# Turned squares of softmax probabilities sent from SBUF straight to SBUF in a fused attention and MLP kernel

## The chip, the cores and the metric

The kernel runs on one core of one Trainium2 chip. The metric is the device time of one execution in microseconds; the time before is the median of three runs.

## The reference

The input is 16 sequences of 256 tokens of width 256. Attention has 16 heads of 128; the MLP is 2048 wide, with 4-bit weights. In the reference's terms:

```python
x = x + layernorm(attention(layernorm(x)))      # causal softmax, 16 heads, biases on q, k, v, out
x = x + layernorm(mlp(layernorm(x)))            # out = (gelu(x Wg) * (x Wu)) Wd

scores = einsum('bqhe,bkhe->bhqk', q, k) / sqrt(128)
attn   = softmax(where(causal, scores, -1e5), axis=-1)
z      = einsum('bkhe,bhqk->bqhe', v, attn)
out    = einsum('bqhe,hed->bqd', z, W_O) + b_O
```

`Wg`, `Wu` and `Wd` are unpacked from 4-bit codes, one scale for every 32 values.

## The kernel before, in words

The 4096 tokens are cut into 8 blocks of 512 (two sequences). Attention goes over *units*: a unit is one block and one head, so there are 128 of them, and two units of neighbouring heads make a *pair* (64 pairs). Almost every product is made of several matmuls on high and low parts of the operands, to keep float32 accuracy.

A software pipeline, written out by hand, is the loop `for i in range(-5, N + 2)` with N = 128. In step `i` these stages are recorded, in this order: `st_s(i+4)` (scores and softmax), `st_qk(i+5)` (keys and queries), `st_t(i+4)`, in the last steps a `part` of the MLP's first group, `st_o` (output projection of an earlier pair), `st_z(i)` (values times probabilities), `st_p(i+1)`, `st_v(i+4)` (values), `st_b(i+3)`, `st_w(i+4)` and then `weights`, which loads weight tiles for later pairs: `wo` and `wv` in odd steps, `wk` and `wq` in even ones. In between, `slot` calls take small jobs from queues: layernorms of other blocks, the splitting of weights, the unpacking of the 4-bit weights.

The helper `run` (line 99) chains every engine instruction behind those recorded before it, and the helper `dma` (lines 86 to 91) does the same for all transfers, which are all issued by SyncE (SP) in the order in which they are recorded. So nothing overtakes on an engine or in SP's queue: a transfer that has to wait holds up all transfers recorded after it. In the built program each transfer also carries one of eight completion counters in turn, and waits until the transfer eight places before it has landed.

The probabilities must be turned (transposed) before `st_z` can use them. For one unit this goes in four stages:

- `st_t`: VectorE transposes the 32 by 32 squares of `pr` into `tr`, 128 partitions by 768 elements.
- `st_w`: `spread` stores `tr` in a DRAM tile `hop`, in four transfers of 32 partitions and 96 KB each. They put the squares where the transposed matrix has them.
- `st_b`: one transfer of 384 KB loads `hop` into the SBUF tile `pt`, of which there are three buffers.
- `st_p`: ScalarE copies the high part `ph` out of `pt`, GpSimd (in the last four units VectorE) makes the low part `pl`. `st_z` reads `ph`, `pl` and a part of `pt` itself on TensorE.

Unit `u` is stored in step `u-4`, loaded in step `u-3`, split in step `u-1` and used in step `u`.

The 4-bit weights are unpacked during attention (`f_make`, `f_scale`) and kept in DRAM (`f_keep`); the second loop, over MLP groups `k`, loads them again (`f_get`). Its tiles are `wg`, `wu` and `wd`. Its first group begins inside the last attention steps.

Of the kernel before, what the change touches and what calls it, by code (L numbers as in the profile page):

```python
# [10 lines left out]
F32 = mybir.dt.float32  # L11
F32R = mybir.dt.float32r
I32 = mybir.dt.int32
BF16 = mybir.dt.bfloat16
AF = mybir.ActivationFunctionType
ALU = mybir.AluOpType

B, S, D, H, E, FF = 16, 256, 256, 16, 128, 2048
P = 128
# [9 lines left out]
def kernel(  # L29
# [19 lines left out]
    nc = tc.nc  # L49
# [4 lines left out]
    wp = ctx.enter_context(tc.tile_pool(name="w", bufs=2))  # L54
    work = ctx.enter_context(tc.tile_pool(name="work", bufs=2))
    small = ctx.enter_context(tc.tile_pool(name="small", bufs=3))
    dram = ctx.enter_context(tc.tile_pool(name="dram", bufs=1, space=bass.MemoryType.DRAM))
    ps = ctx.enter_context(tc.tile_pool(name="ps", bufs=1, space=bass.MemoryType.PSUM))

    def f(ap):  # L60
        return ap.bitcast(F32)
# [24 lines left out]
    def dma(dst, src):  # L86
        if queue[0] is None:
            queue[0] = nc.sync.dma_start(dst, src).ins
            return
        with tc.issue_after(queue[0]):  # L90
            queue[0] = nc.sync.dma_start(dst, src).ins
# [3 lines left out]
    def run(op, dst, *args, **kw):  # L95
        with ExitStack() as behind:
            for m in last.values():
                behind.enter_context(tc.issue_after(m))
            ins = op(dst, *args, **kw)  # L99
        last[ins.ins.engine] = ins.ins  # L100
        return ins
# [3 lines left out]
    V_, G_, A_, N_ = "vgan"  # L105
    urgent, behind, splits, idle, made, spare = (deque() for _ in range(6))
# [91 lines left out]
    def spread(hop, tr):  # L198

        to = hop.rearrange("(k j) a n -> a j k n", k=4)  # L200
        for a in range(4):
            dma(to[a], tr[32 * a : 32 * (a + 1)])
# [161 lines left out]
    N = len(units)  # L364
# [95 lines left out]
    def st_t(u):  # L460


        pr = PR.pop(u)
        tr = work.tile([P, 4, 6, 32], F32, tag="tr", name="tr")
        run(
                nc.vector.transpose,
                tr.rearrange("p k m i -> p m k i"), pr.rearrange("p c b (k j) -> p (c b) k j", k=4)
            )
        TR[u] = tr

    def st_w(u):
        HOP[u] = dram.tile([P, 4, 6 * 32], F32, tag="hop", name="hop", bufs=4)
        spread(HOP[u], TR.pop(u).rearrange("p k m i -> p k (m i)"))

    def st_b(u):

        pt = work.tile([P, 4, 6, 32], F32, tag="pt", name="pt", bufs=3)
        dma(pt.rearrange("p a m i -> p a (m i)"), HOP.pop(u))
        PT[u] = pt

    def st_p(u):
        pt = PT.pop(u).rearrange("p a m i -> p m a i")
        ph = work.tile([P, 2, 2, P], F32R, tag="ph", name="ph")
        pl = work.tile([P, 2, 2, P], F32R, tag="pl", name="pl")
        four = [t.rearrange("p c b (a i) -> p (c b) a i", a=4) for t in (ph, pl)]
        run(nc.scalar.copy, four[0], pt[:, 0:4])

        engine = nc.vector if u >= N - 4 else nc.gpsimd
        run(engine.tensor_tensor, four[1], pt[:, 0:4], f(four[0]), ALU.subtract)
        PH[u] = (ph, pl, pt)  # L490
# [127 lines left out]
    def f_make(g, n, then):  # L618


        pk, sc = LD.pop((g, n))

        def small_tile(dtype, name):
            return work.tile([P, 2, 256], dtype, tag="code", name=name, bufs=3)

        c = work.tile([P, 2, 256], I32, tag="raw", name="codes", bufs=6)
        sg, t = small_tile(BF16, "sg"), small_tile(BF16, "t")
        run(nc.vector.tensor_scalar, c[:, 0, :], pk, 15, None, ALU.bitwise_and)
        run(nc.vector.tensor_scalar, c[:, 1, :], pk, 4, 15, ALU.arith_shift_right, ALU.bitwise_and)
        yield V_  # L630
        if then:
            f_load(*then)
        run(nc.vector.tensor_scalar, sg, c, 8.0, -2.0, ALU.is_ge, ALU.mult)
        yield V_
        run(nc.vector.tensor_scalar, c, c, 7, None, ALU.bitwise_and)
        yield V_
        run(nc.vector.tensor_scalar, t, c, 2.0, 8.0, ALU.mult, ALU.subtract)
        yield V_
        while unscaled:
            step(made)  # L640
        v = small_tile(BF16, "v")
        run(nc.vector.scalar_tensor_tensor, v, c, 0.5, t, ALU.mult, ALU.max)
        yield V_
        run(nc.vector.scalar_tensor_tensor, v, c, 2.0, v, ALU.subtract, ALU.max)
        yield V_
        run(nc.vector.scalar_tensor_tensor, v, sg, 1.0, v, ALU.add, ALU.mult)
        unscaled.append((g, n))
        add(made, f_scale(g, n, v, sc), G_)

    def f_scale(g, n, v, sc):  # L650
        scb = sc.unsqueeze(1).to_broadcast([P, 2, 256])
        if n == "d":
            full = work.tile([P, 2, 256], F32, tag="raw", name="full", bufs=6)
            w = f_tile(n)
            run(nc.gpsimd.tensor_tensor, full, v, scb, ALU.mult)
            unscaled.remove((g, n))
            yield A_
            run(nc.scalar.copy, w[:, 0], full)
            run(nc.gpsimd.tensor_tensor, w[:, 1], full, f(w[:, 0]), ALU.subtract)
        else:  # L660

            full = work.tile([P, 8, P], F32, tag="eight", name="full", bufs=1)
            run(nc.gpsimd.tensor_tensor, full[:, 0:4].rearrange("p (k c) n -> p k (c n)", k=2), v, scb, ALU.mult)
            unscaled.remove((g, n))
            w = f_tile("u")
            yield A_
            run(nc.scalar.copy, w[:, 0, 0:4], full[:, 0:4])
            run(nc.gpsimd.tensor_tensor, w[:, 1, 0:4], full[:, 0:4], f(w[:, 0, 0:4]), ALU.subtract)
            yield G_
            a11, a21, a12, a22, s1, s2, s3, s4 = (full[:, m] for m in range(8))  # L670
            for o, l, r, op in (
                (s1, a21, a22, ALU.add), (s2, s1, a11, ALU.subtract), (s3, a11, a21, ALU.subtract),
                (s4, a12, s2, ALU.subtract),
            ):
                run(nc.gpsimd.tensor_tensor, o, l, r, op)
            yield A_
            run(nc.scalar.copy, w[:, 0, 4:8], full[:, 4:8])
            run(nc.gpsimd.tensor_tensor, w[:, 1, 4:8], full[:, 4:8], f(w[:, 0, 4:8]), ALU.subtract)
        late.append((now[0] + 4, f_keep, (g, n, w)))

    def f_tile(n):
        if n == "d":
            return wp.tile([P, 2, 2, 256], F32R, tag="fd", name="wd", bufs=2)
        if n == "g":
            return wp.tile([P, 2, 1024], F32R, tag="wv", name="wg", bufs=2).rearrange("p s (m c) -> p s m c", m=8)
        return wp.tile([P, 2, 8, P], F32R, tag="fs", name="wu", bufs=2)
# [336 lines left out]
    for i in range(-5, N + 2):  # L1023
        p = i // 2
        odd = i % 2 == 1
        if p >= 0 and not odd and p < len(pairs):
            b, g = pairs[p]
            if g == 0 and b + 1 < NBLK:
                add(urgent, ln1(b + 1), N_)
            if b == 0 and g == 6:  # L1030
                pieces = [(fg, n) for fg in range(NG) for n in "gud"]
                f_load(*pieces[0])
            if b == 0 and g == 7:
                for m, piece in enumerate(pieces):
                    add(idle, f_make(*piece, pieces[m + 1] if m + 1 < len(pieces) else None), V_)
            if b == NBLK - 1 and g == 0:
                add(spare, x_ops(0), N_)
        if 0 <= i + 4 < N:
            st_s(i + 4)
        slot(V_)  # L1040
        if i + 5 < N:
            st_qk(i + 5)
        slot(V_, urgent, behind)
        slot(G_)
        slot(G_)
        if 0 <= i + 4 < N:
            st_t(i + 4)
        if i == N:
            await_(X[0], "last", spare)
            X[0].pop("last")()  # L1050
        if i >= N - 4:
            part(0, ("m1", "m2", "m6", "m5", "m7", "m3")[i - (N - 4)])
        if 0 <= p - 1 < len(pairs):
            st_o(p - 1, i % 2)
        if 0 <= i < N:
            st_z(i)
        if 0 <= i + 1 < N:
            st_p(i + 1)
        if 0 <= i + 4 < N:
            st_v(i + 4)  # L1060
        elif after:
            run(*after.popleft())
        if 0 <= i + 3 < N:
            st_b(i + 3)
        if 0 <= i + 4 < N:
            st_w(i + 4)
        if odd:
            weights((p + 1, "o"), (p + 5, "v"))
        else:
            weights((p + 4, "k"), (p + 4, "q"))  # L1070
        slot(A_ + G_)
        if N - 9 <= i < N - 7:
            f_get(0, "ug"[i - (N - 9)])
# [97 lines left out]
```

## Time and profile before

| | |
|---|---|
| time, median of 3 runs | 1518.19 us (1518.02 to 1520.27) |
| profiled execution, first to last instruction (its span) | 1516.5 us |
| profiled execution's own time outside the span | not recorded apart; the median of the runs is 1.7 us above the span |
| TensorE matmul busy | 1500.2 us, 99% |
| VectorE, ScalarE, GpSimd busy | 1188.5, 1038.3, 724.5 us |
| transfers' share of the 16 DMA engines, 200 to 1000 us | 0.91 to 0.94 |
| the same, 1200 to 1500 us | 0.51 to 0.61 |
| mean granted TensorE clock | 0.998 |

PE is TensorE's matmuls and PEld its weight loads, DVE is VectorE, ACT ScalarE, POOL GpSimd; SPq is SyncE's queue, which issues the transfers. The last attention step's products end at about 1023 us of the span; the MLP goes on to its end. Idle time of an engine that sets no end costs nothing, so the waits that matter here are those of PE.

### The profile page before, as it was taken

To read this page: it belongs to the slowest core of one execution; us is meant where nothing else is said; L and a number is where in the kernel's file an instruction comes from. 1 tells how busy PE (TensorE), PEld (TensorE's weight loads), DVE (VectorE), ACT (ScalarE), POOL (GpSimd) and SP (SyncE) were. 2 spreads that over 40 slices of the span, in tenths; PEclk is the share of its full clock that TensorE was granted. 3 is DMA by queue.
4 is the path that set the end of the run, shared out by engine and by line. 5 is a ranking of instruction groups with operands and counts; after the bars stand their busy time and mean duration, and the time that the engine had idled before them with its cause. 6 is when DMAs were issued, how large, how long until landed. Compare 5 with 4: busy or idle time off the path is not lost.

```text
span 1516.5 us, 25756 instructions
## 1 busy us (share of the span) xinstructions
PE 1500.2 (99%) x7831; PEld 1278.8 (84%) x7831; DVE 1188.5 (78%) x3015; ACT 1038.3 (68%) x2614; POOL 724.5 (48%) x947
## 2 busy tenths in 40 slices
PE   8999999999999999999999999999999999999997
PEld 7888888888888888888888888887888888888886
DVE  6876787787787878788778787777787887787866
ACT  6887776776676677676677767676766665666565
POOL 3754578677767776866876876870000000000000
PEclk9999999999999999999999999999999999999999
DMA  8998899999999899899899999976557465655561
GB/s 289 333 328 260 261 307 305 291 303 313 285 296 322 279 320 309 273 316 302 280 286 320 298 297 318 318 253 259 209 194 261 183 248 196 249 182 196 221 233 58
DMA packets 200426, 407.55 MB, mean 269 GB/s; under 512 B 21472, under 2 KB 128480, under 8 KB 189536
## 3 DMA queue, kind: packets, MB, share of 16 engines
q1 hardware_dynamic: 200288, 405.91, 80.0%
q8 instruction: 62, 1.02, 0.3%
q14 instruction: 76, 0.62, 0.1%
HBM read 294.15 MB, written 111.67 MB: 268 GB/s over the span
## 4 chain that ended last, share of the span: by engine, by line
PE 92%; DVE 2%; DMA 2%; ACT 2%; POOL 1%; issue 1%; SPq 0%; POOLq 0%; DVEq 0%; ACTq 0%
PE pd L99 13%; PE pk L99 11%; PE pv L99 11%; PE pq L99 11%; PE po L99 11%; PE sc L99 9%; PE pz L99 9%; PE pa L99 8%; PE pf L99 5%; PE pe L99 2%; DMA wu<-fu 1%; DVE sum L99 1%; ACT pr L99 0%; DMA rawv<-in_wv 0%; PE warm L99 0%
## 5 line engine op out<-in xcount | busy, mean ns | idle before, releaser
L99 POOL TENSOR_SCALAR pr<-pr,rc 128x128 f32<-128x128 f32 (+1 forms) x512 | 251.1, 508 | 90.1 <-DVE rc L99 90.1
L99 ACT ACTIVATE pr<-sc,mn 128x128 f32<-128x128 f32 (+1 forms) x512 | 208.8, 420 | 87.1 <-DVE mn L99 87.0
L99 POOL TENSOR_TENSOR rs<-rs,mhalf 128x4 f32<-128x4 f32 (+1 forms) x35 | 34.5, 987 | 485.6 <-DVE rs L99 275.7
L99 POOL TENSOR_TENSOR pl<-pt,ph 128x512 fp32r<-128x512 f32 x124 | 160.0, 1290 | 186.5 <-ACT ph L99 178.2
L99 DVE CUSTOM_DVE_ANT_0 sc<-sc,mask 128x128 f32<-128x128 f32 (+1 forms) x512 | 180.7, 373 | 68.0 <-PE sc L99 59.2
L99 PE MATMUL pv<-wv,xT 128*128 128x512 f32 x768 | 208.9, 407 | 0.0
L99 ACT ACTIVATE zh<-pz,bqk 128x512 fp32r<-128x512 f32 x128 | 88.3, 690 | 165.1 <-PE pz L99 165.1
L99 PE MATMUL pk<-xT,wk 128*128 128x512 f32 x768 | 200.3, 396 | 0.3 <-POOL xT L99 0.2
L99 PE MATMUL pd<-inter,wd 128*128 128x512 f32 (+1 forms) x792 | 197.8, 385 | 1.4 <-ACT inter L99 1.0
L99 PE MATMUL pq<-xT,wq 128*128 128x512 f32 x768 | 196.3, 391 | 0.0
L99 PEld LDWEIGHTS pd<-inter,wd 128*128 128x128 f32 x792 | 145.0, 188 | 34.5 <-DVE inter L99 2.9
L99 PEld LDWEIGHTS pq<-xT,wq 128*128 128x128 f32 x768 | 144.2, 188 | 32.9
L99 ACT COPY part<-pa 128x512 f32<-128x512 f32 x192 | 111.9, 586 | 68.4 <-PE pa L99 66.0
L99 PE MATMUL po<-zh,wo 128*128 128x512 f32 x512 | 157.7, 389 | 0.0
L99 PEld LDWEIGHTS pk<-xT,wk 128*128 128x128 f32 x768 | 135.7, 189 | 24.0 <-POOL xT L99 0.7
L99 PEld LDWEIGHTS pv<-wv,xT 128*128 128x128 f32 x768 | 135.0, 189 | 23.6
L99 DVE SCALAR_TENSOR_TENSOR zl<-pz,bqk,zh 128x512 fp32r<-128x512 f32 x128 | 95.8, 749 | 70.5 <-ACT zh L99 70.5
L99 ACT CAST inter<-sum 128x512 fp32r<-128x512 f32 x128 | 80.1, 626 | 87.9 <-DVE sum L99 87.9
L99 DVE TENSOR_TENSOR inter<-sum,inter 128x512 fp32r<-128x512 f32 x128 | 89.0, 695 | 56.9 <-ACT inter L99 56.0
L99 DVE STREAM_TRANSPOSE tr<-pr 128x768 f32<-128x768 f32 x128 | 123.3, 963 | 1.7 <-POOL pr L99 1.2
L99 DVE SCALAR_TENSOR_TENSOR kl<-pk,bqk,kh 128x512 fp32r<-128x512 f32 x128 | 96.1, 751 | 30.9 <-ACT kr L99 27.1
L99 PEld LDWEIGHTS po<-zh,wo 128*128 128x128 f32 x512 | 96.0, 188 | 19.9
(150 smaller groups left out, 3726.1 us busy)
## 6 DMA issues: line engine op xcount, KB each, us to landing
hop<-tr SPq DMA_DIRECT2D x512, 96.0 KB
pt<-hop SPq DMA_DIRECT2D x128, 384.0 KB
wk<-wk SPq DMA_DIRECT2D x64, 512.0 KB
wq<-wq SPq DMA_DIRECT2D x64, 512.0 KB
wo<-wo SPq DMA_DIRECT2D x64, 512.0 KB
wu<-fu SPq DMA_DIRECT2D x32, 1024.0 KB
wg<-fg SPq DMA_DIRECT2D x32, 1024.0 KB
wv<-wv SPq DMA_DIRECT2D x56, 512.0 KB
```

The costliest lines, as they stand in the source:

```text
L99: ins = op(dst, *args, **kw)
```

## The change

The stop in DRAM is removed. `st_b` is gone, `tr` and `pt` hold two units each, and `st_w` is called once a pair, in odd steps, after both units have been turned. It sends sixteen transfers from `tr` to `pt`, each of 32 partitions by 384 elements (48 KB): for every block row `k` of the destination and every block row `a` of the source. To make room, `tr` and `pt` have two buffers of 6 KB a partition (`tr` before: two of 3 KB; `pt`: three of 3 KB), one of three `code` buffers goes, the tag `fd` goes, tiles `wd` that are being made share the two buffers of `fs` with `wu`, and tiles `wd` that are loaded share the two of `pt`.

```diff
         pr = PR.pop(u)
-        tr = work.tile([P, 4, 6, 32], F32, tag="tr", name="tr")
+        if u % 2 == 0:
+            TR[u // 2] = work.tile([P, 4, 2, 6 * 32], F32, tag="tr", name="tr", bufs=2)
...
-    def st_w(u):
-        HOP[u] = dram.tile([P, 4, 6 * 32], F32, tag="hop", name="hop", bufs=4)
-        spread(HOP[u], TR.pop(u).rearrange("p k m i -> p k (m i)"))
-
-    def st_b(u):
-
-        pt = work.tile([P, 4, 6, 32], F32, tag="pt", name="pt", bufs=3)
-        dma(pt.rearrange("p a m i -> p a (m i)"), HOP.pop(u))
-        PT[u] = pt
+    def st_w(p):
+
+        tr = TR.pop(p)
+        PT[p] = work.tile([P, 4, 2, 6 * 32], F32, tag="pt", name="pt", bufs=2)
+        for k in range(4):
+            for a in range(4):
+                dma(PT[p][32 * k : 32 * (k + 1), a], tr[32 * a : 32 * (a + 1), k])
...
-            return work.tile([P, 2, 256], dtype, tag="code", name=name, bufs=3)
+            return work.tile([P, 2, 256], dtype, tag="code", name=name, bufs=2)
...
-        run(nc.vector.tensor_scalar, t, c, 2.0, 8.0, ALU.mult, ALU.subtract)
-        yield V_
         while unscaled:
             step(made)
         v = small_tile(BF16, "v")
-        run(nc.vector.scalar_tensor_tensor, v, c, 0.5, t, ALU.mult, ALU.max)
+        run(nc.vector.tensor_scalar, v, c, 2.0, 8.0, ALU.mult, ALU.subtract)
+        yield V_
+        run(nc.vector.scalar_tensor_tensor, v, c, 0.5, v, ALU.mult, ALU.max)
...
-            w = f_tile(n)
+            w = f_tile(n, True)
...
-    def f_tile(n):
+    def f_tile(n, made=False):
         if n == "d":
-            return wp.tile([P, 2, 2, 256], F32R, tag="fd", name="wd", bufs=2)
+            pool, tag = (wp, "fs") if made else (work, "pt")
+            return pool.tile([P, 2, 2, 256], F32R, tag=tag, name="wd", bufs=2)
...
-        if 0 <= i + 3 < N:
-            st_b(i + 3)
-        if 0 <= i + 4 < N:
-            st_w(i + 4)
+        if 0 <= i + 4 < N and odd:
+            st_w((i + 4) // 2)
         if odd:
             weights((p + 1, "o"), (p + 5, "v"))
```

More of the change, by code (lines that the diff above doesn't have):

```diff
@@ L463, in st_t @@
         pr = PR.pop(u)
-        tr = work.tile([P, 4, 6, 32], F32, tag="tr", name="tr")
-        run(
[L466 to L469, printed above, removed]
-    def st_w(u):
-        HOP[u] = dram.tile([P, 4, 6 * 32], F32, tag="hop", name="hop", bufs=4)
-        spread(HOP[u], TR.pop(u).rearrange("p k m i -> p k (m i)"))
-    def st_b(u):
-        pt = work.tile([P, 4, 6, 32], F32, tag="pt", name="pt", bufs=3)
-        dma(pt.rearrange("p a m i -> p a (m i)"), HOP.pop(u))
-        PT[u] = pt
+        if u % 2 == 0:
+            TR[u // 2] = work.tile([P, 4, 2, 6 * 32], F32, tag="tr", name="tr", bufs=2)
+        run(
+            nc.vector.transpose,
+            TR[u // 2][:, :, u % 2].rearrange("p k (m i) -> p m k i", i=32),
+            pr.rearrange("p c b (k j) -> p (c b) k j", k=4),
+        )
+    def st_w(p):
[4 more added lines that the diff above has]
+                dma(PT[p][32 * k : 32 * (k + 1), a], tr[32 * a : 32 * (a + 1), k])
     def st_p(u):
-        pt = PT.pop(u).rearrange("p a m i -> p m a i")
+        pt = PT[u // 2][:, :, u % 2].rearrange("p a (m i) -> p m a i", i=32)
         ph = work.tile([P, 2, 2, P], F32R, tag="ph", name="ph")
@@ L623, in small_tile @@
         def small_tile(dtype, name):
-            return work.tile([P, 2, 256], dtype, tag="code", name=name, bufs=3)
+            return work.tile([P, 2, 256], dtype, tag="code", name=name, bufs=2)
         c = work.tile([P, 2, 256], I32, tag="raw", name="codes", bufs=6)
-        sg, t = small_tile(BF16, "sg"), small_tile(BF16, "t")
+        sg = small_tile(BF16, "sg")
         run(nc.vector.tensor_scalar, c[:, 0, :], pk, 15, None, ALU.bitwise_and)
```

## The prediction

> **What bounds the kernel now.** I read the busy times and the chain first, then PE's waits, then busy times by stretch, then the order of time where the change acts.
>
> ```profile
> span 1516.5 us, 25756 instructions
> ...
> PE 1500.2 (99%) x7831; PEld 1278.8 (84%) x7831; DVE 1188.5 (78%) x3015; ACT 1038.3 (68%) x2614; POOL 724.5 (48%) x947
> ...
> PE 92%; DVE 2%; DMA 2%; ACT 2%; POOL 1%; issue 1%; SPq 0%; POOLq 0%; DVEq 0%; ACTq 0%
> ```
>
> TensorE is idle for 16.3 us of the span, and the chain runs through it. Its waits:
>
> ```profile
> PE sc L99 <- ACT qr L99: 4.7, 3, 2.6
> PE warm L99 <- POOL ident masks.py:199: 1.6, 1, 1.6
> PE pd L99 <- ACT inter L99: 1.0, 3, 0.4
> ```
>
> None is for `pt` or `hop`. The 4.7 us lie in the first 41 us, where ScalarE is late. By stretch (busy time of PE, PEld, DVE, ACT, POOL, then granted clock, DMA share, GB/s):
>
> ```profile
> 18.40:21.00 2.60, 0.02 (x1) 0.00 (x0) 2.05 (x4) 2.60 (x7) 1.56 (x3) 1.00 0.56 159
> 21.00:25.00 4.00, 3.95 (x15) 3.55 (x16) 3.59 (x13) 2.18 (x9) 0.12 (x1) 0.57 0.86 262
> ...
> 400.00:600.00 200.00, 200.00 (x1121) 173.99 (x1120) 161.04 (x474) 142.50 (x404) 141.04 (x187) 1.00 0.94 303
> ...
> 1200.00:1300.00 100.00, 99.64 (x439) 81.89 (x438) 80.03 (x135) 64.28 (x119) 0.00 (x0) 1.00 0.61 228
> ```
>
> In attention PE has no idle time at a DMA share of 0.94, and a 512-column matmul has a median of 389 ns there (`pq`) as in the MLP (`pd`) at 0.61. So lighter transfers can't quicken PE; a gain could only come out of its idle time. The first two rows show the price of a stall: after 2.6 us without work the clock mean of the next 4 us is 0.57; the clock's records have it at half for 3.4 us.
>
> **What goes.** 128 x (4 stores + 1 load) = 640 transfers. Four stores take 1.96 us to issue (median), a load 0.32: 128 x 2.28 = 292 us of SP. A 768-byte packet of the stores takes 36 ns (median of the packet records), a 3072-byte packet of the loads 121 ns: 65536 x 36 + 16384 x 121 ns = 4.34 ms, or 271 us of 16 engines. All this is beside PE's work, so taking it away is worth 0.
>
> **What comes.** 64 x 16 = 1024 transfers of 48 KB, in 32768 rows of 1536 bytes. Between 46 ns (1024 bytes) and 84 ns (2048) a row takes about 65 ns, an estimate: 133 us of 16 engines. The DMA share in attention falls by some 14 points. SP's time grows. No row shows a transfer from SBUF to SBUF; the nearest are the stores of `hop`, also 32 partitions: 0.48 us from one issue to the next (median; fastest tenth 0.43, slowest 0.85; `xhop`'s fastest tenth 0.35), and the last of four lands 3.05 us after its issue ends (1.6 to 6.1). I take 0.48: 16 x 0.48 = 7.7 us of issue, bounds 5.6 (0.35) and 13.6 (0.85). From the first issue to the last landing that is 7.7 + 3.05 = 10.8 us. A counter serves every eighth transfer, so the ninth of a burst waits for the first; 8 x 0.48 = 3.8 us covers a landing of 3.1.
>
> The rule in the Trainium skill against this change is in DMA: Bandwidth & Descriptors, Rules for kernel authors: many small transfers should be one large one, since under 64 KB one pays mostly overhead. Its fit of 2.0 us plus bytes at 436 GB/s gives 2.1 us for 48 KB, an estimate; sixteen one after another would be 34 us, and no pair would be in time. The rows of `hop`, four issued in 1.96 us, speak for overlap instead.
>
> **Is `pt` in time?** The pair's burst stands in step 2p-3, and `ph` of unit 2p is ScalarE's in step 2p-1.
>
> ```profile
> 609.05 0.32 SPq L91 DMA_DIRECT2D pt<-hop  x1
> 609.46 2.47 SPq L91 DMA_DIRECT2D hop<-tr  x4
> 609.47 0.61 ACT L99 CAST ph<-pt 128x512 fp32r<-128x512 f32 x1
> ```
>
> Three facts of one step: SP is let through here by the products `pz` of this step (as before: the buffer rule for `pt` is the same, its old user is `st_z` of the same step), the squares of the second unit are ready, and `ph` follows each 7.83 us. So from here to `ph` two steps on it is about 15.7 us. Over all pairs, from where the second unit's first store went out to `ph` of the first, I count a median of 14.8 us, a least of 7.7 (last pair) and otherwise at least 10.4. 10.8 fits with 4 us to spare in most steps, and barely in a few; there ScalarE has some 2 us before PE's scores miss it (`ql` ends 2.2 us before the next `sc`). Steady state: 0 (bounds: 0, and from the other rows the rival below). At the start the second unit's squares are ready at 29.2; 29.3 + 10.8 = 40.1 against ScalarE's `ph` at 40.04. ScalarE's late there is PE's late: 0, bounds 0 and 2.
>
> **Who stands behind the burst in SP's queue.** In every odd step the loads `wo` and `wv` follow it, later by 16 x 0.48 - 1.96 - 0.32 = 5.4 us. From `wo`'s landing to PE's first use the trace has a median of 12.1 us and, but for two pairs, at least 5.9. The last two have 0.9 and 5.0. This is the place:
>
> ```profile
> 1007.14 0.98 DVE L99 STREAM_TRANSPOSE tr<-pr 128x768 f32<-128x768 f32 x1 [1.20 <-POOL pr L99]
> ...
> 1008.29 1.85 SPq L91 DMA_DIRECT2D hop<-tr  x4
> 1010.18 0.45 SPq L91 DMA_DIRECT2D wo<-wo  x1
> ...
> 1016.03 0.62 PE L99 MATMUL po<-zh,wo 128*128 128x512 f32 x2
> ```
>
> In these last steps keys, queries and values are done, so a step lasts only 4 us, but the lead of `wo` is still counted in steps. `wo` of pair 62 goes out at 1010.2, lands at 1015.1 by its counter, and PE takes it at 1016.03. After: the last unit's squares are ready at 1008.1, sixteen transfers stand before it, it goes out at 1008.2 + 7.7 = 1015.9 (1013.8 to 1016.8, the latter by the slower tenth without waits, 0.54) and lands 4.4 us on (3.9 to 5.2, least and median of `wo`): 1020.3. PE stands for 1020.3 - 1016.03 = **4.2 us** (1.7 to 6.0). Nothing else is behind this stall: `po` stands before `pz` on PE, and `pz` and the MLP's products follow. The lateness of the last `pt` (1008.2 + 10.8 = 1019.0 against `ph` at 1016.4) goes into the same 4.2 us. Pair 63's `wo` moves from 1013.7 to about 1018.3, lands near 1023, used at 1024.7 plus the stall: 0.
>
> The clock after the stall: 0 (a gap of 1.12 us at 40.2 cost none) to 1.7 us (half of 3.4 us, as after the 2.6 us gap). I take 0.9. TensorE: Matmul & The Clock Gate, Part 1, says that a free-running window of about 3.4 us is judged and an idle one halves the rate. By that alone a stall of 4.2 us could or could not cost 1.7, by its place; the trace's 2.6 us gap was enough.
>
> **The buffers shared.** All engines but SP have the same instructions; one copy of `wd` changes its place on ScalarE and `t` becomes `v` on VectorE: 0. `wd` in `pt`: the first load waits for the products of unit 125, done by 1014.5, and goes out at 1019.4: 0; without that cover each us is one on `wg` behind it. `wu` of the second MLP group now takes the buffer of the last `wd` made, so it waits for the store `fd`, landed at 1022.1; it went out at 1020.7. It landed at 1029.4 behind `wg` (1027.0) and is used at 1030.8, and the stall above gives it 4 us more: 0; if that cover went, about 1.
>
> **The sum** on the span: 0 + 0 + 4.2 + 0.9 = 5.1, 1516.5 to 1521.6. The median of the runs is 1.7 above the span: 1523.3.
>
> **The rivals.** *Hidden* (not slower): the transfers go out every 0.35 us, as `xhop`'s fastest do. Then `wo` goes out at 1008.2 + 5.6 = 1013.8 and lands at 1017.7; the stall is 1.7 with no half clock, 1519.9, and 1518.2 if the landing is quicker too. It decides for spacings under about 0.42 us (stall under 3.0). For it: 48 KB is half of a store, and a load takes 0.32 to issue; against: the median of `xhop` is 0.48 as well. *Every pair late* (slower by far): from a spacing of about 0.86 us on, 16 x 0.86 + 3.05 passes the 14.8 us plus ScalarE's 2 us, and then each us counts 64 times: at 0.9 us 0.6 x 64 = 38 us, 1561 with the end. For it: eight counters and the slowest tenth of the stores at 0.85; against: DMA load falls and these rows carry waits. *Lighter transfers help* (faster): they could only take from PE's waits before 41 us, of which 1.1 us at 40.2 comes after the first `hop`: 1517. Against: that wait is for ScalarE.
>
> **Chances and range.** Stall at the last `wo` 0.55, hidden 0.31, every pair late 0.09, lighter 0.05. A measurement tells 0.2%, 3 us, from no change. The stall case below 3 us counts as same: 0.03 of it; so slower 0.61, same 0.35, faster 0.04 (the lighter case mostly stays within 0.2%, but its chance stands for causes I don't see). The range goes from 1517.8 (hidden) to 1530 (stall 6.0 + 1.7, start 2, and a few late pairs); the steady lateness is left out.
>
> **What would show it.** Right: a wait of PE for DMA `wo` of about 4 us near 1016, SP's sixteen issues in about 7.7 us, no other new wait of PE, attention steps at 7.83 us, a DMA share near 0.8. Wrong: ScalarE waiting for `pt` in many steps, or `wo` landing by 1017.

## The result, and the profile after

The changed kernel takes 1726.16 us (median of 4 runs, 1725.83 to 1728.95) against 1518.11 us before in the same measurement: a ratio of 1.1374, 95% interval 1.1358 to 1.139. The forecast was 1523.3 in a range up to 1530.0, so the time is far outside it. What came is the rival *every pair late*, at five times the price that it was given.

The page of the changed kernel, in the same rows as before (span, busy times, clock and DMA share in 40 slices, the chain):

```profile
span 1724.4 us, 26464 instructions
...
PE 1573.5 (91%) x7831; PEld 1318.7 (76%) x7831; DVE 1198.7 (70%) x3015; ACT 1032.4 (60%) x2614; POOL 721.2 (42%) x947
...
PEclk9998989999988998999899899999899999999999
...
DMA  6766575767667566656766676776665555755552
...
PE 51%; DMA 25%; SPq 16%; DVE 3%; issue 2%; ACT 2%; POOL 1%; POOLq 0%; ACTq 0%; DVEq 0%
```

The span grew by 1724.4 - 1516.5 = 207.9 us. PE does the same 7831 matmuls, but it is idle for 1724.4 - 1573.5 = 150.9 us instead of 16.3 (134.6 more), and the matmuls themselves take 73.3 us longer, because the clock falls to half after stalls: by the clock's records TensorE now loses 77 us of full clock, against 5 before (mean granted clock 0.956 against 0.998). 134.6 + 73.3 is the whole difference. In the chain, transfers (DMA) and SP's own queue (SPq) now hold 41%; they held 2%.

The waits of PE, each with total, number and longest, and below them ScalarE's wait for `pt`, the largest for a transfer on any engine:

```profile
PE po L99 <- DMA wo<-wo: 47.7, 29, 4.9
PE po L99 <- DVE zl L99: 35.5, 7, 5.8
PE sc L99 <- DVE kl L99: 19.6, 7, 4.1
PE sc L99 <- ACT qr L99: 16.8, 9, 4.8
PE pk L99 <- DMA wk<-wk: 10.4, 10, 2.3
```

```profile
ACT ph L99 <- DMA pt<-tr: 151.9, 54, 7.1
```

ScalarE stands 54 times for `pt`, and as engines are in order, all that it does for the next scores and values stands behind that. But PE also waits directly for `wo` and `wk`, loads that stand behind the burst in SP's queue. Both kinds of wait point to SP's queue. By stretch, steady attention and the MLP (columns as before):

```profile
400.00:600.00 200.00, 174.77 (x911) 147.12 (x912) 135.67 (x391) 112.62 (x324) 117.24 (x152) 0.94 0.65 201
...
1400.00:1700.00 300.00, 299.27 (x1315) 245.92 (x1314) 235.25 (x417) 191.35 (x354) 5.04 (x5) 1.00 0.56 207
```

In attention PE did 1121 matmuls in these 200 us before and does 911 now; the engines that move the data are less busy (0.65 against 0.94). In the MLP, where there is no `pt` to turn, PE is still full. Taken over whole pairs, the DMA engines are not what is short. The third view is SP's queue in order of time (start, length, what, how many in a row):

```profile
603.20 0.58 SPq L91 DMA_DIRECT2D wo<-wo  x1
603.82 0.44 SPq L91 DMA_DIRECT2D wv<-wv  x1
604.36 0.38 SPq L91 DMA_DIRECT2D fd<-wd  x1
604.84 0.38 SPq L91 DMA_DIRECT2D wk<-wk  x1
605.30 0.87 SPq L91 DMA_DIRECT2D wq<-wq  x1
606.22 2.02 SPq L91 DMA_DIRECT2D x1d<-xs  x2
608.35 12.05 SPq L91 DMA_DIRECT2D pt<-tr  x16
620.44 0.59 SPq L91 DMA_DIRECT2D wo<-wo  x1
```

The sixteen take 12.05 us, not 7.7. The records of the single transfers show why. The third to eighth of them go out only as the transfers eight places before them land, one after another: `wv` at 609.59, `fd` at 610.83, `wk` at 612.07, `wq` at 613.38, the two `x1d` at 614.05 and 614.81. These are six of the seven transfers of the rows above, from `wv` on, and the DMA engines are moving them at that time. From then on the burst goes at its own pace, 0.63 us apart, each landing about 1.9 us after its issue began. Over all of attention (from the first `pz` to the last), SP stands still for 200.8 us in 204 gaps (of over 0.15 us), each of which ends 16 to 79 ns (median 17) after the transfer eight places ahead has landed; in other gaps it stands for 53 us. In the kernel before it was 58.8 us in 94 gaps, with 344 us in others: there SP had time to spare.

And this is the price of one stall, on PE at 608.2 (start, length, and in brackets the idle time before and what ended it) and by the clock in 2 us stretches:

```profile
608.20 0.73 PE L99 MATMUL po<-zh,wo 128*128 128x512 f32 x2 [2.19 <-DMA wo<-wo]
```

```profile
606.00:608.00 2.00, 0.01 (x1) 0.00 (x0) 1.17 (x5) 2.00 (x10) 2.00 (x2) 1.00 0.87 205
608.00:610.00 2.00, 1.80 (x6) 1.48 (x7) 1.45 (x4) 1.23 (x4) 2.00 (x5) 0.79 0.98 356
610.00:612.00 2.00, 2.00 (x10) 1.90 (x10) 0.98 (x1) 0.00 (x0) 2.00 (x3) 0.50 1.03 422
612.00:614.00 2.00, 2.00 (x12) 1.74 (x10) 0.75 (x1) 1.20 (x2) 0.84 (x2) 0.86 1.03 380
614.00:616.00 2.00, 2.00 (x15) 1.84 (x14) 1.35 (x7) 0.75 (x2) 2.00 (x2) 1.00 0.61 172
616.00:618.00 2.00, 2.00 (x11) 1.65 (x10) 1.68 (x7) 2.00 (x9) 1.15 (x4) 1.00 0.34 85
```

A gap of 2.19 us is followed by granted clocks of 0.79, 0.50 and 0.86: about 0.42 + 1.0 + 0.28 = 1.7 us lost on top of the 2.19. By the matmul records PE has 47 gaps of over 1 us (2 before), 28 of them over 2 us (1 before), the wait before its very first matmul not counted.

The same rows show loads and burst taking turns. While the burst waits for its counters, the DMA engines are full with the loads that went out in a bunch before it (shares 0.98 to 1.03, all sixteen busy); once the burst runs, the share falls to 0.34.

### The profile page after: what moved, and what is told of

Read it like the earlier page. It is cut to its first block, busy times and chain, and to the rows that moved or that the text cites. A ratio compares the mean times of both kernels' runs of the same rounds, so it can differ in the third digit from the quotient of the medians.

```text
span 1724.4 us, 26464 instructions
## 1 busy us (share of the span) xinstructions
PE 1573.5 (91%) x7831; PEld 1318.7 (76%) x7831; DVE 1198.7 (70%) x3015; ACT 1032.4 (60%) x2614; POOL 721.2 (42%) x947
## 3 DMA queue, kind: packets, MB, share of 16 engines
q8 instruction: 63, 1.03, 0.2%
## 4 chain that ended last, share of the span: by engine, by line
PE 51%; DMA 25%; SPq 16%; DVE 3%; issue 2%; ACT 2%; POOL 1%; POOLq 0%; ACTq 0%; DVEq 0%
SPq L91 16%; PE pd L99 12%; DMA wq<-wq 8%; PE pa L99 7%; PE po L99 5%; PE pf L99 5%; PE pv L99 5%; PE pz L99 5%; PE pk L99 4%; PE sc L99 4%; PE pq L99 4%; DMA xr<-xhop 3%; DMA xs<-in_x 3%; DMA wo<-wo 3%; PE pe L99 2%
## 5 line engine op out<-in xcount | busy, mean ns | idle before, releaser
L99 POOL TENSOR_SCALAR pr<-pr,rc 128x128 f32<-128x128 f32 (+1 forms) x512 | 246.9, 498 | 105.0 <-DVE rc L99 105.0
L99 PE MATMUL pv<-wv,xT 128*128 128x512 f32 x768 | 220.1, 423 | 0.6 <-DMA wv<-wv 0.6
L99 PE MATMUL pk<-xT,wk 128*128 128x512 f32 x768 | 210.3, 411 | 10.6 <-DMA wk<-wk 10.4
L99 PE MATMUL po<-zh,wo 128*128 128x512 f32 x512 | 166.5, 407 | 47.8 <-DMA wo<-wo 47.7
L99 PE MATMUL pq<-xT,wq 128*128 128x512 f32 x768 | 200.8, 397 | 6.0 <-DMA wq<-wq 5.9
L99 PEld LDWEIGHTS pk<-xT,wk 128*128 128x128 f32 x768 | 141.9, 197 | 38.2 <-DMA wk<-wk 13.3
L99 ACT CAST ph<-pt 128x512 fp32r<-128x512 f32 x128 | 79.8, 623 | 152.5 <-DMA pt<-tr 151.9
L99 PEld LDWEIGHTS pv<-wv,xT 128*128 128x128 f32 x768 | 142.5, 199 | 26.4 <-DMA wv<-wv 1.3
L99 PE MATMUL po<-zl,wo 128*128 128x512 f32 x256 | 105.3, 411 | 35.5 <-DVE zl L99 35.5
L99 DVE RECIPROCAL rc<-sm 128x2 f32<-128x2 f32 x256 | 41.4, 162 | 131.4 <-ACT pr L99 128.7
```

## The experiments

The theory after the comparison, called A: a transfer in SP's queue can't go out before the one eight places in front of it has landed; large loads take longer to land (medians of the changed kernel 3.5 us for `wo`, 5.3 `wv`, 6.2 `wk`, 7.8 `wq`, against 2.0 for the burst's transfers); so a burst of sixteen behind large loads is held up, and with it all that stands behind it. Rivals: the way from SBUF to SBUF is slow in itself (B); the shared buffers or the pairs cost the time (C); it is the mere number of transfers, whatever they carry (D, H); the sheer delay of `wo` and `wv` behind the burst (E); others named where they come up. Beside each experiment the kernel before was timed on the same chip, at about 1519 us; ratios are to that. "SP stands for counters" below means what the 200.8 us above mean: gaps in attention that end as the transfer eight places ahead lands.

**1. Pairs and shared buffers, but through DRAM** (four stores and one load a pair).

```diff
...
+        spread(HOP[p], TR.pop(p).rearrange("p k u n -> p k (u n)"))
+
+    def st_b(p):
+
...
-        for k in range(4):
-            for a in range(4):
-                dma(PT[p][32 * k : 32 * (k + 1), a], tr[32 * a : 32 * (a + 1), k])
+        dma(PT[p].rearrange("p a u n -> p a (u n)"), HOP.pop(p))
...
+        if 0 <= i + 3 < N and not odd:
+            st_b((i + 3) // 2)
```

> Pairs, shared buffers and two-unit tiles as after the change, but the stop in DRAM is kept: per pair four stores of 192 KB in the odd step and one load of 768 KB in the next even step (5 transfers a pair instead of 16). Theory A (SP's queue: sixteen issues at 0.63 us and the eight counters put the burst and the weight loads in series, 19.2 us a pair against PE's 15.7): 1515 to 1530, no wait of PE for a weight tile. Rival C (the shared buffers or the two-unit grain cost the time): 1650 to 1730.

Measured: 1530.7 us, ratio 1.0068 (1.0052 to 1.0085). C falls as the main cause: this kernel, with the shared buffers and the grain of pairs, is some 12 us slower than the kernel before. PE's busy time from 1000 to 1100 us, at the hand-over from attention to the MLP, is 47.18 + 46.97 = 94.2 us against 99.0 before; the first 1000 us lose 2.7. SP stands 42.2 us for counters.

**2. The kernel before, its four stores of a unit cut into eight.**

```diff
-        spread(HOP[u], TR.pop(u).rearrange("p k m i -> p k (m i)"))
+        tr = TR.pop(u).rearrange("p k m i -> p k (m i)")
+        to = HOP[u].rearrange("(k j) a n -> a j k n", k=4)
+        for a in range(4):
+            for h in range(2):
+                dma(to[a][:, 2 * h : 2 * h + 2], tr[32 * a : 32 * (a + 1), 2 * h : 2 * h + 2])
```

> The kernel before with each store of hop cut in two: eight stores of 48 KB and one load per unit, so 18 transfers a pair for the turned squares, but nine in each step. Theory A: 9 x 0.48 = 4.3 us of SP a step of 7.83, the loads land meanwhile: 1515 to 1530. Rival D (the number of small transfers alone makes it slow): 1650 or more. Rival B (the way from SBUF to SBUF is what is slow): 1518.

Measured: 1667.0 us, ratio 1.0985 (1.0949 to 1.102). A's number was missed and D's held: the old way, the old buffers, the same bytes and the same steps, and cutting the stores alone costs 148 us. It did not fit A as I had put it, with one burst of sixteen as the culprit; eight stores and a load are already more than eight places. SP stands 271.0 us for counters here, against 58.8 in the kernel before. What waits is telling: PE for `wk`, 70.9 us, and SP for the landing of the 384 KB load `pt`:

```profile
PE pk L99 <- DMA wk<-wk: 70.9, 33, 6.5
```

```profile
SPq L91 <- DMA pt<-hop: 87.3, 117, 2.4
```

**3. The burst in two halves**, eight transfers in the odd step and eight in the next even one.

```diff
...
-        for k in range(4):
+        for k in range(2 * part, 2 * part + 2):
             for a in range(4):
...
         if 0 <= i + 4 < N and odd:
-            st_w((i + 4) // 2)
+            st_w((i + 4) // 2, 0)
+        if 0 <= i + 3 < N and not odd:
+            st_w((i + 3) // 2, 1)
```

> After the change, but the sixteen transfers are sent eight in the odd step and eight in the next even step. Theory A: 8 x 0.63 = 5.0 us of SP a step, two weight loads behind them, whose landings are waited for only by the seventh and eighth transfer of the next step: 1530 to 1600. Rival B (the way from SBUF to SBUF): as after, 1700 to 1740. Rival D (the number): as after too.

Measured: 1636.7 us, ratio 1.077 (1.0754 to 1.0786). Between the two expectations. Spreading the same sixteen over two steps gives back 89 of the 208 us; SP still stands 109.7 us for counters.

**4. `wo` and `wv` recorded in front of the burst of the same step.**

```diff
-        if 0 <= i + 4 < N and odd:
-            st_w((i + 4) // 2)
         if odd:
             weights((p + 1, "o"), (p + 5, "v"))
...
+        if 0 <= i + 4 < N and odd:
+            st_w((i + 4) // 2)
```

> After the change, but in odd steps wo and wv are issued before the sixteen transfers. Theory A (everything in series on one queue): 1660 to 1730, PE's waits for wo go and waits for wk, wq or late pt take their place. Rival E (the prediction's mechanism alone, wo behind the burst): PE's 48 us of waits for wo and the half clock after them go, 1640 or less, and no other wait grows.

Measured: 1726.0 us, ratio 1.1354 (1.1315 to 1.1394): no gain, so E falls. `wo` is no longer late, but the loads now stand directly in front of the burst, its eighth transfer waits for them in all 56 pairs that I counted in mid-attention, and PE waits for `ph` instead (40.4 us, 22 times). SP stands 240.5 us for counters.

**5. No reloads of the attention weights** from block 2 on.

```diff
+            if n == "v":
+                W[p // 2, n] = W[2 + p // 2 % 2, n]
+            else:
+                W[p, n] = W[6 + p % 2, n]
+        elif False:
             if n == "v":
```

> After the change, but from the second block on the attention weights are not loaded again (each pair uses one of the last two sets of the first block, so heads get the wrong weights): 224 loads of 512 KB are left out. Theory A (burst and loads in series): the sixteen issues alone are 10.1 us of a pair's 15.7: 1525 to 1560 (the first block still has its stores). Rival B (the way from SBUF to SBUF is slow by itself): 1690 or more. Rival F (SP's issue time alone, 0.63 us each, with everything else that SP issues): 1690 or more, as SP has only 2 us less a pair to issue.

Measured: 1546.0 us, ratio 1.0175 (1.0151 to 1.0199). The sixteen transfers, 0.63 us apart, are all there, and 180 of the 208 us are gone. SP stands 17.8 us for counters. B falls as the main cause. By stretch:

```profile
0.00:200.00 200.00, 181.48 (x977) 154.56 (x977) 132.21 (x388) 135.47 (x379) 98.77 (x147) 0.97 0.58 184
200.00:400.00 200.00, 200.00 (x1128) 174.18 (x1127) 161.58 (x468) 139.11 (x395) 147.50 (x192) 1.00 0.44 122
400.00:600.00 200.00, 199.77 (x1119) 173.54 (x1118) 161.77 (x467) 140.15 (x400) 140.02 (x185) 1.00 0.39 109
```

In the first 200 us, where these kernels still load and split the first weights, PE loses 11.8 us of busy time against before (193.29); after that it is as full as before. Where no large loads share the queue, the change costs PE nothing between 200 and 1000 us, as forecast.

**6. The reloads issued by ScalarE**, out of SP's order; the eight counters are common to both queues in the built program.

```diff
...
+            side[0] = nc.scalar.dma_start(dst, src).ins
...
-                dma(f(w[:, part]), WD[key % (NG // 2), n][:, part])
+                dma_side(f(w[:, part]), WD[key % (NG // 2), n][:, part])
...
-                dma(f(w), WD[p % NG, n])
+                dma_side(f(w), WD[p % NG, n])
```

> After the change, but the reloads of the attention weights are issued by ScalarE, not by SP (the eight counters stay common). Theory A with the order of the queue as its main part: 1540 to 1620; with the counters as its main part: 1650 to 1740, since ScalarE then waits for counters too. Rival B: 1700 or more.

Measured: 1661.9 us, ratio 1.0915 (1.0869 to 1.0961). Taking four issues a pair off SP brings 64 us; the larger part stays. ScalarE also waits more for its own work now (PE's wait for `qr` is 56.0 us), so the time alone did not prove the counters. The records do show their hold: SP stands 178.1 us for counters, and 94.1 us of it (52 gaps) end as a transfer lands that ScalarE has issued, which is not in SP's queue at all.

**7. Sixteen small stores, but to DRAM**, then the one load of experiment 1.

```diff
...
+        to = HOP[p].rearrange("(k j) a n -> k j a n", k=4)
         for k in range(4):
             for a in range(4):
-                dma(PT[p][32 * k : 32 * (k + 1), a], tr[32 * a : 32 * (a + 1), k])
+                dma(to[k][:, a], tr[32 * a : 32 * (a + 1), k])
...
+        dma(PT[p].rearrange("p a u n -> p a (u n)"), HOP.pop(p))
```

> As the kernel with pairs and the stop in DRAM, but with sixteen stores of the same 32 x 384 shape as the changed kernel's transfers, and one load. Theory A: the burst is as long as its issue spacing makes it: at 0.48 us 7.7 us, at 0.63 us 10.1, with one transfer more a pair: 1600 to 1760. Rival B (SBUF to SBUF): the same shape to DRAM is quick, 1515 to 1540.

Measured: 1705.5 us, ratio 1.123 (1.1203 to 1.1258). With experiment 1 this is the cleanest pair: the same kernel, four stores or sixteen, 1530.7 or 1705.5. It is the sixteen, wherever they go. Here one store follows another by 0.47 us (median), the spacing that I had forecast, and it does not help. SP stands 284.9 us for counters. The load stands behind the stores, and ScalarE waits for it in 63 of the 64 pairs (354.7 us), so that part of this loss may be the longer way and not the queue.

**8. The sixteen issued by GpSimd**, with eight counters of its own.

```diff
...
+            ins = nc.gpsimd.dma_start(dst, src).ins
...
-                dma(PT[p][32 * k : 32 * (k + 1), a], tr[32 * a : 32 * (a + 1), k])
+                dma_gp(PT[p][32 * k : 32 * (k + 1), a], tr[32 * a : 32 * (a + 1), k])
```

> After the change, but GpSimd issues the sixteen transfers, with eight counters of its own. Theory A: SP is left with the loads alone; if GpSimd can issue sixteen in its idle time of about 8 us a pair: 1515 to 1560; if an issue takes GpSimd 1 us or more, pl and the probabilities are late instead: 1600 to 1800, with no wait of PE for weights. Rival B: 1700 or more with pt landing late although issued early.

Measured: 1938.9 us, ratio 1.2769 (1.2749 to 1.2789). It tells nothing on the counters: GpSimd itself becomes late. The busy times on its page, and PE's main wait:

```profile
PE 1642.3 (85%) x7831; PEld 1372.2 (71%) x7831; DVE 1183.5 (61%) x3015; ACT 1030.1 (53%) x2614; POOL 1202.7 (62%) x1971
```

```profile
PE pz L106 <- DVE zl L106: 185.6, 50, 7.3
```

1024 transfers added 1202.7 - 721.2 = 481.5 us to POOL, 0.47 us each.

**9. The reloads issued by GpSimd**: as experiment 6, but four transfers a pair now use other counters than the sixteen.

```diff
-            side[0] = nc.scalar.dma_start(dst, src).ins
+            side[0] = nc.gpsimd.dma_start(dst, src).ins
```

> The changed kernel, but the reloads of the attention weights (some 3.9 a pair) are issued by GpSimd, which has eight completion counters of its own; the sixteen transfers stay on SyncE. Theory A (a short transfer has to wait for the landing of the transfer eight places before it, and large loads among those eight land in 5 to 9 us): the short ones now follow only short ones and a few others, so they go out every 0.63 us and land in 2 to 4 us; pair period back near 15.7 us, 1535 to 1600, the upper part because each issue takes GpSimd about 0.5 us in line with its other work. Rival G (the counters are not it; short transfers are slow because large ones use the DMA engines at the same time, as when ScalarE issued the reloads): 1640 to 1700, with short landings still above 4 us. If GpSimd stands waiting for weight buffers, PE waits on zl or pl and the time says nothing on either.

Measured: 1603.28 us, ratio 1.055 (1.0535 to 1.0566), 3 us above what A expected, and 59 us better than by ScalarE. GpSimd pays 117 us of busy time for it. SP stands 99.5 us for counters, 48.0 of them for the burst's own transfers. What A had wrong is the landing: the small transfers still land in 4.2 us (median), as G said, against 1.9 where the large loads are left out (experiment 5).

**10. As experiment 5, but each reload left as a 2 KB load in its place in the queue.**

```diff
+            tiny = work.tile([P, 4], F32, tag="tiny", name="tiny", bufs=4)
+            dma(tiny, WD[p // 2 % (NG // 2) if n == "v" else p % NG, n][:, 0, :4])
+            if n == "v":
+                W[p // 2, n] = W[2 + p // 2 % 2, n]
...
```

> The changed kernel, but each reload of the attention weights from block 2 on is replaced by a load of 2 KB into a spare tile, in the same place of SyncE's queue; the first blocks' weights are used on. The number of transfers stays at some 23 a pair, only the bytes of the large ones go. Theory A (count times landing, shared by at most eight): landing falls to about 2.5 us, 23.2 x 2.5 / 5.5 = 10.5 us, under PE's 15.7, so 1535 to 1570, and much as when the reloads were left out altogether (1546). Rival H (it is the number of transfers that SyncE has to issue, whatever they carry): 1640 to 1730.

Measured: 1549.94 us, ratio 1.0199 (1.0182 to 1.0216), practically experiment 5. D and H fall: 23.2 transfers a pair, as many as in the changed kernel, nearly fit if all of them land quickly. SP stands 15.8 us for counters. SP's queue in it:

```profile
574.77 1.65 SPq L91 DMA_DIRECT2D tiny<-wo  x1
576.47 0.43 SPq L91 DMA_DIRECT2D tiny<-wv  x1
576.95 0.94 SPq L91 DMA_DIRECT2D xs<-in_x  x2
577.93 0.47 SPq L91 DMA_DIRECT2D tiny<-wk  x1
578.44 0.43 SPq L91 DMA_DIRECT2D tiny<-wq  x1
...
581.59 10.21 SPq L91 DMA_DIRECT2D pt<-tr  x16
```

The same order, the same number, and the sixteen take 10.21 us, about 16 x 0.63.

**11. Experiments 9 and 3 together.**

> Both at once: reloads issued by GpSimd, and the sixteen transfers sent as eight in the odd and eight in the next even step. Theory A: if the shared counters were the cost, what is left is small, and the finer grain can only help the other loads behind the burst: 1525 to 1590, not above the kernel with reloads on GpSimd alone. Rival G: about the split alone, 1620 to 1650. If GpSimd is held up by weight buffers, both kernels of this call show it alike.

Measured: 1619.24 us, ratio 1.0667 (1.0643 to 1.0691): 16 us above experiment 9, so A's "not above" was missed. The second half of the squares goes out a step later, nearer to its use, and ScalarE's wait for `pt` is 147.7 us (38 times) against 68.5 (24 times). With the loads out of SP's queue, the early burst is the better one; splitting helped only where loads stood behind the burst.

No variant beats the kernel before; the nearest is experiment 1, the old way through DRAM in pairs, 0.7% slower.

## Why the prediction failed, step by step

The step that failed is **"Is `pt` in time?"**, which put the steady state of the sum at 0; it measured 3.26 us a pair, 209 us in all. Its criterion, time from the first issue to the last landing against a median margin of 14.8 us, is needed but not enough: by it alone the 14.7 us measured would still fit as a median. Here are its terms, measured in the issue and counter records of 56 bursts of mid-attention (p10 and p90 bound the fastest and the slowest tenth):

| | forecast | changed kernel, median | reloads left out (5), median |
|---|---|---|---|
| sixteen issues | 7.7 us (16 x 0.48) | 13.4 (p10 11.7, p90 15.5) | 10.6 |
| then until the last has landed | 3.05 | 1.3 | 1.3 |
| first issue to last landing | 10.8 | 14.7 (p90 16.9) | 12.0 |

- **Spacing, 0.48 us.** Unhindered it is 0.63 (issue 0.59), so 10.1 us for sixteen. I took the nearest row, the stores of `hop`; the same shape to DRAM does go at 0.47 (experiment 7). This part of the error, 2.4 us, would have cost little by itself: in experiment 5 the 12.0 us fit.
- **"The ninth waits for the first; 8 x 0.48 covers a landing of 3.1."** This is what cost most of the 208 us. The count started inside the burst. But the first eight transfers also have eight in front of them, and these are the large loads of the same pair, which I had listed in the queue as victims and not as a cause. The gaps of over 0.7 us lie almost all at the second to eighth transfer: in 46 of the 56 bursts the eighth was held up, the ninth in 2. That is 3.5 us a burst, and a mean of 3.1 us a pair in gaps that end as a counter's transfer lands.
- **Who stands behind.** I moved `wo` by 5.4 us and looked for the stall only at the last pairs. The check that was missing is the sum of SP's queue over one pair: 13.4 us for the burst and some 7 other transfers at about 0.5 us make 17 us, more than the 15.7 us of two attention steps, before any wait for squares or buffers is added. SP has become the bound. A pair takes 18.55 us (products to products, over all 64) against 15.29: 64 x 3.26 = 209 us, the whole loss. By the records of SP, the 18.55 us are these, beside the kernel with 2 KB loads (experiment 10), which has the same transfers in the same order:

| us a pair, mean over attention | changed kernel | 2 KB loads (10) |
|---|---|---|
| SP issues (gaps up to 0.15 us included) | 14.6 | 14.8 |
| SP stands until a counter's transfer has landed | 3.1 | 0.2 |
| SP stands for anything else | 0.8 | 0.7 |
| sum, and the pair's time | 18.55 | 15.8 |

  The issues alone leave about one us of the 15.7 free, and only the standing for counters differs.
- **The rival "every pair late"** was the case. Its deciding point, a spacing of 0.86 us, wasn't far off: the burst averages 13.4 / 16 = 0.84, and 0.97 in its slowest tenth. Its price was far off: 38 us at 0.9 counted only the lateness of `pt`, neither the queue behind it nor the clock, which costs 73 us by itself. Its chance of 0.09 was too low, because the eight counters that I named for it were checked only against the burst.
- **The end of attention.** A stall of 4.2 us for the last `wo` was forecast; the trace has two, 9.5 us in all, the longer 4.9. Mechanism right, size doubled, and a twentieth of the loss.
- **The buffers shared, 0.** Together with the grain of pairs some 12 us (experiment 1), not separated further.
- **Lighter transfers don't quicken PE**: right. Experiment 5 has a DMA share of 0.39 and PE is as full, and no fuller, than at 0.94 before.
- **The half clock**: right in kind, 1.7 us after a gap of 2.19 us. The Trainium skill (TensorE: Matmul & The Clock Gate, Why this matters for your kernels) warns of idle gaps over about 3 us; here a shorter one, 2.19 us, was enough.

The rule of the Trainium skill that was weighed against the change (DMA: Bandwidth & Descriptors, Rules for kernel authors, on many small transfers) pointed the right way. The 34 us that the prediction set beside it did not come: that was sixteen times the page's fit, which the page measured on transfers issued by GpSimd, while these are SP's. Sixteen in a row took 10.1 us to issue where nothing held them up, and most of the loss went when the loads in front of them were made short (experiment 10). The same section (Rules for kernel authors) says that spreading transfers over issuing engines doesn't help bandwidth and saves only issue time. Here SP's issuing was what was short, and moving four loads a pair off SP gained 64 us by ScalarE and 123 by GpSimd.

**What stays open.** Experiments 6 and 9 differ in the counters, but also in the engine that issues, so the 59 us between them are not proven to be the counters alone. That the first eight transfers of a burst go out as those in front land is seen in the records. But experiments 5 and 10 take away the large loads' traffic together with their hold on the counters; how much of the loss is left when only the hold goes was not separated (in experiment 9 the counters are apart, the small transfers still land late, and the last landing of a burst comes 15.7 us after its first issue, as a median). Nor is it shown what part of the loss in experiment 7 is the queue.

## What to carry to other kernels

Cut a transfer into more only after adding up the issuing queue over one period of the loop: issues, and for each the landing of the transfer that held its completion counter before it, large loads of other stages included. A lower mean share of the DMA engines says nothing about it: here it fell from 0.94 to 0.65 while the kernel lost 14%. If small transfers must be many, keep them away from large loads in the same rotation of counters; and in a kernel that keeps PE full, price each stall with the half clock behind it.

## What the runs showed of the hardware

- A transfer of 32 partitions x 384 elements from SBUF to SBUF takes SP 0.59 us to issue, 0.63 from one to the next, and lands 1.9 us after its issue began when the large loads are left out (experiment 5); the same shape to DRAM takes 0.42, 0.47 and 1.7, beside the large loads (experiment 7).
- A 1536-byte packet from SBUF to SBUF takes 98 ns (median; least 62) in the changed kernel and also without the large loads (experiment 5), where the prediction put about 65; to DRAM it takes 74 (median, experiment 7).
- A transfer issued by GpSimd costs it about half a us of busy time: 481.5 us for 1024 small ones (experiment 8), 117 for 224 loads (experiment 9).
